# Two graph-attention layers: early row gathers for two chunks, and layer 2 in rounds with one hold of GpSimd

## The chip, the cores and the metric

One core of a Trainium2 chip runs the kernel. Its engines are TensorE (PE, with its weight loads PEld), VectorE (DVE), ScalarE (ACT), GpSimd (POOL) and SyncE (SP); 16 DMA engines move data. The metric is the device time of one execution in microseconds, the median of several.

## The reference

A graph has N = 6250 nodes with 128 features and E = 106250 edges, sorted by destination. Two transformer convolutions with H = 2 heads are computed, with a batch norm and a relu between them, then a residual and a layer norm:

```python
rel_t_enc = jnp.cos((last_update[src] - t)[:, None] * time_w + time_b)
edge_attr = jnp.concatenate([rel_t_enc, msg], axis=-1)        # 32 + 64
def conv(h, ...):
    q, k, v = h @ Wq + bq, h @ Wk + bk, h @ Wv + bv           # (n, 2, 64) each
    e = edge_attr @ We
    alpha = sum(q[dst] * (k[src] + e)) / sqrt(64)             # for each edge and head
    a = exp(alpha - max over dst) / (sum over dst)
    return segment_sum((v[src] + e) * a, dst) + h @ Ws + bs
h = relu(batchnorm(conv(x)))
return layernorm(x + conv(h))
```

## The kernel before

The edges are cut into NC = 104 chunks of 1024 (T = 8 tiles of 128), and each layer goes over the chunks once. A **plan** stage first makes tables of the indices (the source columns `srcs`, the destination columns, the weight columns), checks that the input has the form that the fast path wants, writes the features with their node times as rows `xv_d` to DRAM, and makes block 0 of the tables of layer 1 (`ftab`: query times key weight for each node and head, L630, L636, L638). Then **layer 1**, the statistics of the batch norm, and **layer 2** run, both through the function `conv`.

A chunk passes these stages. *fetch* (SP's queue): attributes of the edges (L781), the four pieces of the table for the chunk's nodes (L797), and others (L803 to L807), behind up to four register loads (L777). *gather* (POOL): 8 indirect DMAs, one for each tile of 128 source rows (L815), from `xv_d` in layer 1 and from `hn_d` in layer 2. *encode* (layer 1): the cosines of the edge's times on DVE and ACT (L853 to L872). *turn_in*: PE transposes the rows (L885, in layer 1 the attributes too, L894), ACT copies them out (L889, L895). *score*: products with the table (L916). *lowest*: DVE finds the greatest exponent (L924, L926). *weigh*: ACT's exp (L931). *turn_weights*: 3 transposes (L940) and a copy (L941). *gather_sums*: 24 matmuls add the weighted rows up (L956) into the bank `fpa`, which comes from a pool of two. *divide*: DVE (L963 to L968). *finish_turn*: two matmuls (L978, L979) into the other half of the same bank and a copy `fat` (L981). *product*: with the value weights (L987, L988; in layer 2 L993, L994), into that half again. *complete*: the residual (L1032, reading `fpa`) and the layer norm (L1032 to L1043); *store* scales the rows (L1049) and sends them out (L761).

The order on every engine is the order of the code. A round k of layer 2 holds, on PE: score(k), product(k-3), turn_weights(k-1), finish_turn(k-2), turn_in(k+1), a piece of other work (later blocks of tables, L630, or of the features, L1219, or the residual, L1299), gather_sums(k-1). DVE does divide(k-2), lowest(k), complete(k-3) and the copy of the time attributes (L1141); ACT does weigh(k) and the copies. The 8 gathers of chunk k+3 are spread over the round: each has a hold, a wait for a step of PE that stands close before it in the code (`behind`, L817 to L819): the end of gather_sums, the score, turn_weights, finish_turn, the two halves of turn_in, and two steps within gather_sums. A gather's rows go into a buffer `ff` of a pool (7 in layer 1, 6 in layer 2). Layer 1 has the same rounds with a lead of four chunks.

Before layer 1's first round, `turn_features` (L656 to L662) transposes all features, 49 transposes in 13 blocks, into `xT`. The first gathers wait for the writing of `xv_d`.

Of the kernel before, what the change touches and what calls it, by code (L numbers as in the profile page):

```python
# [7 lines left out]
F32 = mybir.dt.float32  # L8
# [56 lines left out]
SWITCH = NC - 3  # L65
STARTS = (*range(0, NC - 2, LG), NC - 2, NC - 1)
# [3 lines left out]
def general(ctx: ExitStack, tc: tile.TileContext, x, src, dst, edge_attr_64, edge_weight, node_vec,  # L70
# [95 lines left out]
    step = RW * GT * (-(-64 // GT))  # L166
# [147 lines left out]
    def conv(c, kv_d, qt_d, agg_d):  # L314
        we = wt[c][4]
        w = 2 * D + (c == 1)
        with ExitStack() as cs:
            load = cs.enter_context(tc.tile_pool(name=f"load{c}", bufs=3))
# [217 lines left out]

def room(nc, pl, const, c, w, brief=None):
# [108 lines left out]
def turn_features(nc, pl, mp, N):  # L646
# [5 lines left out]
    for b0 in range(0, NF, 4):  # L652
        n = min(4, NF - b0)
        px = mp.tile([P, 4, P], F32, name="fpx")
        for i in range(n):
            nc.tensor.transpose(px[:, i], pl.rows[:, b0 + i, 1:], pl.ident)  # L656
        eng = nc.scalar.copy if b0 // 4 % 2 else nc.vector.tensor_copy
        eng(lanes[:, b0:b0 + n], px[:, :n])
    if N > NF * P:
        px = mp.tile([P, 4, P], F32, name="fpx")  # L660
        nc.tensor.transpose(px[:, 0], pl.rest[:, 1:], pl.ident)
        nc.vector.tensor_copy(xT[:, NF * P:N], px[:, 0, :N - NF * P])  # L662
# [3 lines left out]
def ordered(ctx: ExitStack, tc: tile.TileContext, pl, x, dst, edge_attr_64, conv2, bn_g, bn_b, out):  # L666
# [9 lines left out]
    const = ctx.enter_context(tc.tile_pool(name="fconst", bufs=1))  # L676
    dram = ctx.enter_context(tc.tile_pool(name="fdram", bufs=1, space=bass.MemoryType.DRAM))
# [51 lines left out]
    AHEAD = 4  # L729

# [9 lines left out]
    def conv(c, extra, first_blocks=None):  # L740
# [9 lines left out]
        p_a = cs.enter_context(tc.tile_pool(name=f"fp_a{c}", bufs=2, space=bass.MemoryType.PSUM))  # L750
        pl.bank = lambda: p_tr.tile([P, GE], F32, name="fpg", tag="tr")

        together = mybir.DependencyInfo(mybir.DependencyClass.Sync, mybir.DependencyReason.DATA)
# [14 lines left out]
        def fetch(k):  # L768
# [9 lines left out]
            s.f = f = load.tile([P, T, FW], F32, name="ff")  # L778
# [22 lines left out]
            if c:  # L801
# [4 lines left out]
                s.r = load.tile([NN, D], F32, name="fr", bufs=7)  # L806
# [3 lines left out]
        def gather(k, rows, behind=None):  # L810
            f = ch[k].f
            for t in rows:
# [31 lines left out]
        def encode(k):  # L844
# [8 lines left out]
            nc.vector.tensor_sub(rel, s.f[:, :, 0], pl.ew[:, :, k])  # L853
# [90 lines left out]
        def gather_sums(k):  # L944
# [3 lines left out]
            s.po = bank[:, 1].rearrange("p (i n) -> p i n", i=2)  # L948
# [35 lines left out]
        def product(k):  # L984
            po, at = ch[k].po, ch[k].at
            if c == 0:
                nc.tensor.matmul(po[:, 0], wv[c], at[:, 0], start=True, stop=False)  # L987
                nc.tensor.matmul(po[:, 0], web[c], at[:, 1], start=False, stop=True)  # L988
                return
            at = at.rearrange("p i (n h) -> p i n h", h=H)  # L990
            for h in range(H):
                r = slice(h * C, (h + 1) * C)
                nc.tensor.matmul(po[:NN, 0, r], at[:, 0, :, h], wv[c][:, r], start=True, stop=False)  # L993
# [566 lines left out]
```

## Time and profile before

| | us |
|---|---|
| median of 3 runs (lowest, highest) | 2671.73 (2668.62, 2673.74) |
| the profiled execution | 2670.95 |
| its span, first to last instruction | 2669.1 |
| granted TensorE clock, mean | 0.879 |
| first gather | 33.6 |
| first score of layer 1 | 87.1 |
| first gather of layer 2 | 1351.4 |
| last lowest (L924) of layer 2 | 2650.7 |

In the profile's lines, an engine's line of code, operation and tiles come first (`ff<-hn_d,fsrcs` writes ff from hn_d by the indices fsrcs). In a group stand the count, the busy time in all, the mean time of one in ns, and the idle time of the engine ahead of these instructions with what ended it. On a timeline stand the start, the time, the engine and the instructions, and in brackets the idle time before; "issue" means that nothing that the profile shows was waited for. A row of a stretch has the busy time of PE, PEld, DVE, ACT and POOL, then the granted clock, the share of the DMA engines and GB/s.

### The profile page before, as it was taken

The numbers are of one execution on the slowest core, as the hardware profiler recorded it, in microseconds if no ns is written. First come the engines' busy times: TensorE is split into PE (matmuls) and PEld (weight loads), VectorE is DVE, ScalarE is ACT, GpSimd is POOL, SyncE is SP. The second block draws the span as 40 slices with busy tenths as digits, with TensorE's granted clock in tenths as the row PEclk, the third lists the DMA queues.
The fourth block names the chain that finished last, engine by engine and source line by source line (L and its number), as shares of the span: only waits on it lengthen the run. The fifth ranks groups of instructions, "written<-read, shape, count | busy, mean of one in ns | idle before, by whom it ended". The sixth has DMA issues, their size and how long they took to land. (4 is left out here: it accounts for less than half of the span.)

```text
span 2669.1 us, 50291 instructions
## 1 busy us (share of the span) xinstructions
PE 1851.4 (69%) x14961; PEld 1107.9 (42%) x14961; DVE 1148.0 (43%) x3998; ACT 1082.5 (41%) x1906; POOL 1588.3 (60%) x1684
## 2 busy tenths in 40 slices
PE   3677767777777677677746667676767767676666
PEld 2444444444444444444424334444444434443443
DVE  3555555555555555565625222333232322232223
ACT  1455545553434444454532333333333333333333
POOL 4466666666666666666345666666666666666662
PEclk8799889988989989889977888888888898888888
DMA  6455555555555555555447555555555555555542
GB/s 177 128 148 146 146 153 145 144 143 151 146 147 138 152 148 145 144 144 138 126 118 194 148 140 148 152 153 147 143 150 148 157 147 142 154 143 140 128 134 52
DMA packets 535244, 383.29 MB, mean 144 GB/s; under 512 B 405638, under 2 KB 479258, under 8 KB 531634
## 3 DMA queue, kind: packets, MB, share of 16 engines
q1 hardware_dynamic: 460998, 231.66, 33.4%
q0 software_dynamic: 53184, 109.45, 17.1%
q10 hardware_dynamic: 20780, 38.87, 3.9%
q8 instruction: 122, 2.00, 0.3%
q14 instruction: 160, 1.31, 0.2%
HBM read 267.85 MB, written 108.49 MB: 141 GB/s over the span
## 5 line engine op out<-in xcount | busy, mean ns | idle before, releaser
L815 POOL DMA_INDIRECT ff<-xv_d,fsrcs x831 | 795.1, 957 | 511.2 <-issue 166.2
L815 POOL DMA_INDIRECT ff<-hn_d,fsrcs x783 | 743.6, 950 | 453.3 <-issue 172.3
L941 ACT COPY fpt<-fppt 128x384 f32<-128x384 f32 x208 | 99.6, 479 | 1261.9 <-PE fpx L885 705.6
L916 PE MATMUL fps<-fft,ftab 128*32 128x384 f32 (+2 forms) x2080 | 406.2, 498 | 146.5 <-issue 64.5
L956 PE MATMUL fpa<-ff,fpt 128*32 128x225 f32 x5008 | 350.6, 419 | 120.0 <-DVE fres L1032 102.2
L924 DVE TENSOR_REDUCE flow<-fps 128x1 f32<-128x384 f32 x208 | 116.1, 558 | 587.6 <-PE fpx L885 352.7
L885 PE MATMUL fpx<-fident,ff 128*128 128x128 f32 x1664 | 276.9, 299 | 38.5 <-issue 25.8
L956 PEld LDWEIGHTS fpa<-ff,fpt 128*32 128x32 f32 x5008 | 167.6, 125 | 321.0 <-issue 233.7
L916 PEld LDWEIGHTS fps<-fft,ftab 128*32 128x32 f32 x2080 | 142.7, 124 | 323.6 <-issue 161.8
L894 PE MATMUL fpe<-fident,ff 128*112 128x128 f32 x832 | 142.4, 295 | 189.0 <-issue 184.3
L889 ACT COPY fft<-fpx 128x512 f32<-128x512 f32 x404 | 232.2, 575 | 45.7 <-remote 20.1
L885 PEld LDWEIGHTS fpx<-fident,ff 128*128 128x128 f32 x1664 | 221.0, 156 | 54.5 <-issue 36.1
L916 PE MATMUL fps<-fxT,ftab 112*32 112x384 f32 (+2 forms) x1040 | 218.4, 509 | 17.2 <-issue 16.8
L963 DVE TENSOR_SCALAR finv<-fpa 128x1 f32<-128x1 f32 x208 | 32.0, 154 | 446.8 <-PE fps L916 237.6
L916 PE MATMUL fps<-fet,ftab 112*32 112x384 f32 (+2 forms) x1040 | 167.4, 448 | 33.0 <-issue 32.7
L894 PEld LDWEIGHTS fpe<-fident,ff 128*112 128x112 f32 x832 | 97.1, 141 | 218.6 <-issue 213.1
L978 PE MATMUL fpa<-fsel,fa 128*128 128x128 f32 x416 | 103.3, 332 | 81.5 <-DVE fsel L968 46.5
L860 DVE SCALAR_TENSOR_TENSOR farg<-fturns,farg 128x256 f32<-128x256 f32 x312 | 132.9, 426 | 10.7
L895 ACT COPY fet<-fpe 112x512 f32<-112x512 f32 x208 | 124.6, 599 | 9.9 <-PE fps L916 2.8
L940 PE MATMUL fppt<-fident,fs 128*128 128x128 f32 x626 | 117.1, 296 | 13.4 <-issue 5.8
L931 ACT ACTIVATE fs<-fps,fm 128x384 f32<-128x384 f32 x208 | 120.5, 579 | 9.7 <-DVE fm L926 6.1
L867 ACT ACT_TABLE_LOAD x82 | 105.2, 1283 | 42.2 <-issue 34.7
(224 smaller groups left out, 2654.4 us busy)
## 6 DMA issues: line engine op xcount, KB each, us to landing
ff<-in_edge_attr SPq DMA_DIRECT2D x206, 256.0 KB
et_d<-fet SPq DMA_DIRECT2D x104, 448.0 KB
fxT<-et_d SPq DMA_DIRECT2D x104, 448.0 KB
tab_d<-fo ACTq DMA_DIRECT2D x26, 1024.0 KB
ftab<-tab_d SPq DMA_DIRECT2D x832, 32.0 KB
enc_d<-fzs SPq DMA_DIRECT2D x104, 128.0 KB
fz<-enc_d SPq DMA_DIRECT2D x104, 128.0 KB
ff<-xv_d,fsrcs POOLq DMA_INDIRECT x831
```

The costliest lines, as they stand in the source:

```text
L815: row = nc.gpsimd.indirect_dma_start(out=f[:, t, (1 if c else 0):1 + D], out_offset=None, in_=(h_d[:N, :] if k < RAW else hn_d) if c else ...
L860: nc.vector.scalar_tensor_tensor(arg, turn, -part, arg, op0=OP.mult, op1=OP.add)
L867: nc.scalar.activation(z[:, :len(of)], arg[:, :len(of)], AF.Sin, bias=qpi)
L885: last = nc.tensor.transpose(px[:, t * P:(t + 1) * P], s.f[:, u * 4 + t, 1:1 + D], ident)
L889: nc.scalar.copy(s.ft[:, u * GE:(u + 1) * GE], px)
L894: last = nc.tensor.transpose(pe[:EC, t * P:(t + 1) * P], s.f[:, u * 4 + t, 1 + D:], ident)
L895: nc.scalar.copy(s.et[:, u * GE:(u + 1) * GE], pe[:EC])
L916: steps.append(nc.tensor.matmul(s.ps[r, to:to + n], s.tab[:kd, r, i], (of.et if i else of.ft)[:kd, at:at + n], start=i == 0, stop=i == 1))
L924: nc.vector.tensor_reduce(low, s.ps, AX.X, OP.min)
L931: nc.scalar.activation(s.s[:, :s.ps.shape[1]], s.ps, AF.Exp, bias=s.bias, scale=-1.0)
L940: last = nc.tensor.transpose(pp[:, t * P:(t + 1) * P], s.s[:, t * P:(t + 1) * P], ident)
L956: steps.append(nc.tensor.matmul(s.pa[r], s.pt[:, t * P + g * GH:t * P + (g + 1) * GH], f[:, i % T, 1:1 + D + EW], start=t == 0, stop=t == ...
```

## The change

**First part: the start.** The 16 gathers of chunks 0 and 1 take their rows directly from the input `x` into two buffers that are kept (`ffe`), as soon as the source columns are there. These rows have no node time in them, so `early_times` works the times out: the source index is split into a slot of 64 nodes and a place in it; a wide matmul spreads the indices over the partitions, ACT and DVE make a one-hot of the slot, four narrow matmuls fetch the slot's 64 times, and DVE picks the place. It stands between the steps of the tables' block 0. The check of the plan comes earlier, and a set of columns comes last. `turn_features` is now taken in pieces by layer 1: 3 blocks in each of the two rounds before the first score and 7 in round 0. In layer 1, gathers up to round 2 have no holds.

On PE this is the start of the program before, from the transpose of the features' first block to the first score (`fx`: features of block 0, `fm`, `fws`: weights of the tables, `fhT`: the features as loaded).

```order
L1513 MATMUL fpx<-fident,fx_234 128x128 x4
L630 MATMUL fpx<-fxT_318,fm_273 128x512
L630 MATMUL fpx<-fxT_318,fm_281 128x512
L630 MATMUL fpx<-fxT_318,fm_289 128x512
L630 MATMUL fpx<-fxT_318,fm_297 128x512
L630 MATMUL fpx<-fxT_318,fws_107 128x512
L1433 MATMUL fpx<-fident,erows 128x104 x8
L1525 COMPARE_AND_BRANCH
L656 MATMUL fpx<-fident,fhT 128x128 x48
L661 MATMUL fpx<-fident,fxrest 128x128
L885 MATMUL fpx<-fident,ff 128x128 x4
```

And on PE after, first the plan from its last table step, then the first stages of layer 1 (`ffe`: the rows gathered from x).

```order
L567 MATMUL fpx<-rowf,frow 98x512
L573 MATMUL fpx<-fslots,fnear 128x64 x4
L673 MATMUL fpx<-fxT_336,fws_109 128x512
L1544 MATMUL fpx<-fident,erows 128x104 x8
L1544 MATMUL fpx<-fident,rowf 128x104 x8
L1646 COMPARE_AND_BRANCH
L699 MATMUL fpg<-fident,fhT 128x128 x12
L935 MATMUL fpx<-fident,ffe_75 128x128 x4
L944 MATMUL fpe<-fident,ffe_75 112x128 x4
L699 MATMUL fpg<-fident,fhT 128x128 x12
L966 MATMUL fps<-fft,ftab 32x384 x4
```

The steps of the early times (L567, L573) stand between those of the tables (L673, before L630), and of the features' 49 transposes (L699, before L656) 24 stand ahead of the first score (L966, before L916).

**Second part: layer 2.** For rounds 0 to 96 the new function `steady` takes every stage's input from a round before: in round k, PE does gather_sums(k-2), score(k), product(k-4), a piece of other work, turn_weights(k-1), finish_turn(k-3), turn_in(k+1); DVE does lowest(k-1), divide(k-3), complete(k-5), and the copy of the attributes last; ACT does weigh(k-1). `catch_up` then does the stages that lag, and the last rounds run in nearly the old order. The bank `fpa` of gather_sums comes from a pool of one in layer 2, and finish_turn and product use a bank `fpo` of their own. The `ff` are a ring of 7, shared by both layers, with the two `ffe` in it.

On PE this is a round of layer 2 before, from the end of the score(k):

```order
L916 MATMUL fps<-fxT,ftab 32x256
L993 MATMUL fpa<-fwv_121,fat 64x64
L994 MATMUL fpa<-fwe_124,fat 64x64
L993 MATMUL fpa<-fwv_121,fat 64x64
L994 MATMUL fpa<-fwe_124,fat 64x64
L940 MATMUL fppt<-fident,fs 128x128 x3
L978 MATMUL fpa<-fsel,fa 128x128
L979 MATMUL fpa<-fsel,fa 128x128
L885 MATMUL fpx<-fident,ff 128x128 x8
L1299 MATMUL fpg<-fws_125,fhT 128x128 x4
L956 MATMUL fpa<-ff,fpt 32x225 x12
```

And a round after, from the end of the score to gather_sums of the next round:

```order
L966 MATMUL fps<-fxT,ftab 32x256
L1044 MATMUL fpo<-fwv_125,fat 64x64
L1045 MATMUL fpo<-fwe_128,fat 64x64
L1044 MATMUL fpo<-fwv_125,fat 64x64
L1045 MATMUL fpo<-fwe_128,fat 64x64
L1407 MATMUL fpg<-fws_129,fhT 128x128 x4
L990 MATMUL fppt<-fident,fs 128x128 x3
L1029 MATMUL fpo<-fsel,fa 128x128
L1030 MATMUL fpo<-fsel,fa 128x128
L935 MATMUL fpx<-fident,ff_470 128x128 x8
L1007 MATMUL fpa<-ffe_76,fpt 32x225
L1007 MATMUL fpa<-ff_468,fpt 32x225 x11
```

The row of matmuls is nearly the same; what moved is the chunk that each belongs to, the piece of other work (L1299, after L1407), and that product and finish_turn (`fpo`) no longer share gather_sums' bank (`fpa`).

On POOL, this is one chunk's gathers before, each with the semaphores that it waits for (`DMASW`: an earlier gather's landing; `PE`: its hold):

```order
L815 DMA ff<-hn_d,fsrcs 128x128 [waits DMASW7_49,DMAHW4_49,DVE_49,PE_49]
L815 DMA ff<-hn_d,fsrcs 128x128 [waits DMASW0_49,PE_49]
L815 DMA ff<-hn_d,fsrcs 128x128 [waits DMASW1_49,PE_49]
L815 DMA ff<-hn_d,fsrcs 128x128 [waits DMASW2_49,PE_49]
L815 DMA ff<-hn_d,fsrcs 128x128 [waits DMASW3_49,PE_49]
L815 DMA ff<-hn_d,fsrcs 128x128 [waits DMASW4_49,PE_49]
```

And one chunk's gathers after:

```order
L865 DMA ff_469<-hn_d,fsrcs 128x128 [waits DMASW7_49,PE_49]
L865 DMA ff_469<-hn_d,fsrcs 128x128 [waits DMASW0_49]
L865 DMA ff_469<-hn_d,fsrcs 128x128 [waits DMASW1_49]
L865 DMA ff_469<-hn_d,fsrcs 128x128 [waits DMASW2_49]
L865 DMA ff_469<-hn_d,fsrcs 128x128 [waits DMASW3_49]
L865 DMA ff_469<-hn_d,fsrcs 128x128 [waits DMASW4_49]
```

Only the first gather of a chunk still waits for PE: the last transpose of turn_in in the round before. The core of the diff:

```diff
+STEADY = NC - 8
+EARLY = 2
-def turn_features(nc, pl, mp, N):
+def turn_features(nc, pl, N):
...
-            s.f = f = load.tile([P, T, FW], F32, name="ff")
+            s.f = f = pl.ffs[k % len(pl.ffs)]
...
+            if not c and k < EARLY:
+                return
...
-            s.po = bank[:, 1].rearrange("p (i n) -> p i n", i=2)
+            s.po = joined[:, :2] if c else bank[:, 1].rearrange("p (i n) -> p i n", i=2)
+            s.product = joined[:NN, 2] if c else s.po[:, 0]
...
+        def steady(k, held):
+            fetch(k + lead(k))
+            gather(k + lead(k), range(T), held)
+            if on(k - 1):
+                lowest(k - 1)
+            if on(k - 3):
+                divide(k - 3)
+            if on(k - 1):
+                weigh(k - 1)
+            if on(k - 5):
+                complete(k - 5)
+            if on(k - 2):
+                gather_sums(k - 2)
+            score(k)
+            if on(k - 4):
+                product(k - 4)
...
+            if on(k - 1):
+                turn_weights(k - 1)
+            if on(k - 3):
+                finish_turn(k - 3)
+            turn_in(k + 1, 0)
+            held = turn_in(k + 1, 1)
...
+            attributes(k)
+            if done:
+                store(*done.pop(0))
+            return held
+
+        def catch_up(k):
+            lowest(k)
+            weigh(k)
+            for j in (k - 4, k - 3, k - 2):
+                while done:
+                    store(*done.pop(0))
+                if j == k - 2:
+                    divide(j)
+                    finish_turn(j)
+                (complete if j == k - 4 else finish)(j)
+            gather_sums(k - 1)
...
+                if c and 0 <= k <= STEADY:
+                    held = steady(k, held)
+                    if k == STEADY:
+                        catch_up(k)
+                    continue
```

More of the change, by code (lines that the diff above doesn't have):

```diff
@@ L1102, in conv @@
                     lowest(k)
[L1103 removed]
+                if not c and on(k - 3) and k <= SWITCH:
                     complete(k - 3)
@@ L1361, in tile_gnn_resnorm @@
         nc.gpsimd.memset(got.hT[:, N // P * (1 + D):], 0.0)
+        got.early = [keep.tile([P, T, FW], F32, name=f"ffe{k}") for k in range(EARLY)]
         got.rest = keep.tile([P, 1 + D], F32, name="fxrest")
@@ L1505, in tile_gnn_resnorm @@
         nc.vector.tensor_scalar(oki, tot, 0.0, None, op0=OP.is_equal)
-        columns(drows, dsts)
-        for _ in matrices(nc, got, 0, keep, bank, pl):
+        rows(nc.scalar, erows, edge_weight, CE)
+        for _ in made_ready:
             pass
+        next(timed)
         codes(nc, got, keep, mw, bank)
```

133 lines of the change are left out of this document (100 added, 33 removed).

## The prediction

> **What bounds the kernel now.** I read the page first, then the table of stretches, then the groups of instructions and the waits of one long stretch of layer 2, then single rounds on the timeline. The page gives the span and says that no engine is busy all the time.
>
> ```profile
> span 2669.1 us, 50291 instructions
> PE 1851.4 (69%) x14961; PEld 1107.9 (42%) x14961; DVE 1148.0 (43%) x3998; ACT 1082.5 (41%) x1906; POOL 1588.3 (60%) x1684
> ```
>
> The run that was profiled took 2670.95 us, 1.85 more than its span, and lies 0.78 below the median of 2671.73. I make the sum against 2670.95 and add the 0.78 at the end. Layer 2 is even in itself, as this stretch of 300 us shows (busy PE, PEld, DVE, ACT, POOL, then clock, DMA share and GB/s):
>
> ```profile
> 1700.00:2000.00 300.00, 209.20 (x1715) 124.49 (x1716) 89.14 (x360) 106.29 (x228) 185.94 (x197) 0.88 0.56 148
> ```
>
> PE is busy 70% and POOL 62%, and DVE, ACT and the DMA engines have room. What a round costs on each engine is in the groups between 1450 and 2600 us:
>
> ```profile
> L815 POOL DMA_INDIRECT ff<-hn_d,fsrcs x756 | 717.3, 949 | 433.3 <-issue 166.1 <-PE fps L916 89.9 <-remote 58.4
> L924 DVE TENSOR_REDUCE flow<-fps 128x1 f32<-128x384 f32 x94 | 52.4, 558 | 243.4 <-PE fpx L885 125.7 <-PE fpg L630 49.4 <-remote 41.5
> L916 PE MATMUL fps<-fft,ftab 128*32 128x384 f32 (+1 forms) x939 | 206.1, 508 | 104.5 <-issue 37.1 <-ACT fspare L1042 26.9 <-ACT fft L889 23.2
> L916 PE MATMUL fps<-fxT,ftab 112*32 112x128 f32 (+2 forms) x943 | 200.7, 504 | 16.8 <-issue 16.3
> L956 PE MATMUL fpa<-ff,fpt 128*32 128x225 f32 x2256 | 145.9, 391 | 118.6 <-DVE fres L1032 101.4 <-issue 16.8 <-DVE fmean L1033 0.4
> L885 PE MATMUL fpx<-fident,ff 128*128 128x128 f32 x752 | 125.4, 318 | 12.0 <-issue 7.4 <-PE fpa L979 2.1 <-DMA ff<-hn_d,fsrcs 1.3
> L993 PE MATMUL fpa<-fwv,fat 128*64 128x64 f32 x376 | 64.0, 246 | 33.9 <-issue 33.2
> L994 PE MATMUL fpa<-fwe,fat 128*64 128x64 f32 x376 | 57.4, 237 | 29.1 <-issue 29.1
> ```
>
> flow stands once in a round, so 94 rounds took 1150 us: **12.23 us a round**. A round holds 8 gathers of 0.949 us busy. Between two gathers that wait for nothing lie 0.30 us (the timeline below), so 8 gathers need 8 x 1.25 = 10.0 us, and 2.2 us of the round are GpSimd waiting, mostly for the step of PE behind which a gather is held. PE in turn idles in front of gather_sums (118.6 us, of which 101.4 for fres, the last reader of the bank) and of the score (104.5 us). So neither engine is full. They wait for each other in turn, and that is what one hold with stages a round apart could take out: at most 2.2 us a round.
>
> **What speaks for a smaller gain.** PE does not work at one speed. This is a quiet round, from 2042.8 us, with GpSimd waiting at its end (PE first, then POOL):
>
> ```profile
> 2042.80 0.33 PE L993 MATMUL fpa<-fwv,fat 128*64 128x64 f32 x2
> 2043.21 0.28 PE L994 MATMUL fpa<-fwe,fat 128*64 128x64 f32 x2
> 2044.26 1.04 PE L885 MATMUL fpx<-fident,ff 128*128 128x128 f32 x8
> 2045.22 1.35 PE L956 MATMUL fpa<-ff,fpt 128*32 128x225 f32 x24
> ```
>
> Product, turn_weights, finish_turn and turn_in follow each other without a gap and are done in 2.5 us. Now the same work in the round after, beside nine gathers without a pause and a tenth:
>
> ```profile
> 2045.72 1.06 POOL L815 DMA_INDIRECT ff<-hn_d,fsrcs  x1 [2.21 <-PE fpx L885]
> ...
> 2055.83 0.94 POOL L815 DMA_INDIRECT ff<-hn_d,fsrcs  x1 [0.30 <-issue]
> 2057.68 0.94 POOL L815 DMA_INDIRECT ff<-hn_d,fsrcs  x1 [0.92 <-issue]
> 2060.72 0.94 POOL L815 DMA_INDIRECT ff<-hn_d,fsrcs  x1 [2.10 <-PE fpx L885]
> ```
> ```profile
> 2056.01 0.37 PE L885 MATMUL fpx<-fident,ff 128*128 128x128 f32 x1 [1.06 <-issue]
> 2056.72 0.37 PE L885 MATMUL fpx<-fident,ff 128*128 128x128 f32 x1 [0.34 <-issue]
> 2058.14 0.37 PE L885 MATMUL fpx<-fident,ff 128*128 128x128 f32 x1 [1.04 <-issue]
> ```
>
> Transposes that wait for nothing ("issue") start 0.7 or 1.4 us apart instead of 0.13, and GpSimd then waits 2.10 us for the last of them. A product of 8 matmuls shows the same where it begins late in a run of gathers; this one, 4.6 us into the run that began at 2072.71, takes 3.24 us to its last start, against 0.47 above:
>
> ```profile
> 2077.32 0.33 PE L993 MATMUL fpa<-fwv,fat 128*64 128x64 f32 x2
> 2078.41 0.29 PE L994 MATMUL fpa<-fwe,fat 128*64 128x64 f32 x2 [0.76 <-issue]
> ...
> 2080.55 0.27 PE L994 MATMUL fpa<-fwe,fat 128*64 128x64 f32 x1 [0.45 <-issue]
> ```
>
> So from about the fourth gather of an unbroken run on, PE's sequencer gets its instructions slowly. How slowly on the whole, the groups of L993 and L994 tell: 33.9 + 29.1 = 63 us of idle time, in 94 products, of which I counted 33 on the timeline that begin in the fourth or fifth gather of a run. 63/33 = 1.9 us each and the 0.47 are 2.4 us, **0.3 us a matmul**; the transposes above are at 0.7. Why, the trace does not say. Today the holds break runs up. The change makes all runs eight long.
>
> **The change, part by part.**
>
> *Layer 2, 97 rounds.* No stage is removed; each round has the same matmuls, gathers and loads, so the worth is in waits alone. Let the hold fall at 0, behind the last transpose. gather_sums has one bank now and must wait until divide of the chunk before has read it. DVE runs, behind finish_turn, the copy fat, the attributes, flow with fm, and three steps of divide:
>
> ```profile
> L981 DVE COPY fat<-fpa 128x256 f32<-128x256 f32 x94 | 37.9, 403 | 2.7 <-PE fpx L885 1.6 <-PE fpg L630 0.8 <-PE fpa L956 0.4
> L1141 DVE COPY ff<-fz 128x256 f32<-128x256 f32 x95 | 27.7, 291 | 0.0
> L966 DVE TENSOR_SCALAR fa<-fpa,finv 128x225 f32<-128x225 f32 x94 | 42.6, 454 | 3.3
> L963 DVE TENSOR_SCALAR finv<-fpa 128x1 f32<-128x1 f32 x94 | 14.9, 158 | 404.2 <-PE fps L916 215.9 <-remote 132.5 <-PE fpa L994 46.3
> ```
>
> 0.40 + 0.29 + 0.56 + 0.45 + three small ones of 0.16 = 2.2 us, of which turn_in covers 1.0: a wait of 0 to 1.2 us (0 if turn_in is slow). Then gather_sums 1.2 us (next start less own) and the score, 20 matmuls of (206.1 + 200.7)/1882 = 0.22 us, so about 2.2 to 4.3 us; with its inputs a round old I take the lower end, since its waits for fft and fspare go. That is 3.4 to 4.6 us into the run of gathers, the point from which PE slows. What is left is product 8, turn_weights 3, finish_turn 2 and turn_in 8 matmuls, 21, and in most rounds one or two of the tables of later rows, 23 in all: 3 us at the quiet rate, 23 x 0.3 = 7 us at the slow one, 16 us at 0.7. Round by the three: 10.0 (GpSimd is longer), 10.4 to 11.6, and above 19, which the end of the gathers at 10.0 cuts off, since PE then speeds up again. The trace has one direct likeness, the run above: 8 x 1.25 and a wait of 2.10 in place of the gap of 0.30 is 11.8. I take **11.6**, near the likeness and the top of the middle. 97 x (11.6 - 12.23) = **-61 us**. Bounds: 10.0 (-216) and 13.1 (+84, below). The gathers that lose their holds cost nothing themselves. Other queues are spared: SP's loads keep three rounds of lead, and the seven row buffers are free two rounds before they are gathered into.
>
> DVE's copy of the attributes (L1141) now runs just as the gathers start. The Trainium skill (SBUF — State Buffer, Who interferes with whom) says that such a DVE copy locks GpSimd out while it runs; by that rule up to 0.29 us a round, 28 us, would be added. The 756 gathers average 949 ns with 95 such copies among them, so the sum has nothing for it.
>
> *The start.* Before, the 28 gathers from 33.6 us on run unbroken while the turned features are made, and PE stops in the middle of them:
>
> ```profile
> 33.61 1.11 POOL L815 DMA_INDIRECT ff<-xv_d,fsrcs  x1 [30.16 <-DMA fwv<-in_L_gnn_Wv]
> ```
> ```profile
> 35.59 4.51 PE L630 MATMUL fpx<-fxT,fm 128*128 128x512 f32 x6 [0.78 <-DVE fxT L1515]
> ...
> 68.38 1.97 PE L656 MATMUL fpx<-fident,fhT 128*128 128x128 f32 x8 [17.04 <-issue]
> 73.99 5.38 PE L656 MATMUL fpx<-fident,fhT 128*128 128x128 f32 x24 [3.64 <-ACT fxT L658]
> ...
> 87.12 1.51 PE L916 MATMUL fps<-fft,ftab 128*32 128x384 f32 x8
> ```
>
> With 16 gathers done earlier, the two idle times of 17.04 and 3.64 should go: -20.7. The 25 transposes moved behind the first score are paid there, at no gain or loss. The early times add 4 matmuls as wide as L630's (4.51/6 = 0.75 us each) and 16 narrow ones (0.13 to 0.2), with their DVE steps: 5 to 6 us in a chain where PE is waiting part of the time. I charge 6: **-15 us**. Bounds -21 (hidden) and +6 (the 16 gathers stall the plan instead; the DMA engines are fuller there):
>
> ```profile
> 12.00:33.00 21.00, 9.74 (x45) 7.59 (x45) 12.15 (x59) 2.87 (x7) 0.00 (x0) 1.00 0.89 280
> ```
>
> *Entry and end of layer 2.* Chunks 0 to 3 of layer 2 are gathered without a hold before and in round 0, much as now: 0, give or take 12. The end makes up two more rounds of product, a finish_turn and a gather_sums at once, 0.5 x 2 + 0.4 + 1.2 and their DVE: **+4** (2 to 8).
>
> **The sum.** -61 - 15 + 4 = -72: 2670.95 - 72 = 2599, and 2600 beside the median.
>
> **The rivals.**
>
> *GpSimd sets the pace.* PE is not slowed by runs of eight, or it is ahead by then. For it: the quiet rows need 3.4 + 3 = 6.4 us, far below 10. Against it: the slow rows. At 10.3 us a round (10.0 and 0.3 for the hold) 97 x -1.93 = -187, with -11 for the rest: 2474. The Trainium skill (SBUF — State Buffer, Who interferes with whom) states that a DMA never contends with a compute engine, which would give this time; the transposes 0.7 us apart beside the gathers speak against it here.
>
> *The runs of eight starve PE.* Nothing of the last 23 matmuls gets through before the gathers end, so every round is 10.0 + 23 x 0.13 = 13.1: +84 - 11 = 2744, **slower**. It decides when a round passes 12.23 + 11/97 = 12.34 us, that is when PE has more than 2.3 us of work left at the last gather. For it: in the run of 28 gathers at the start PE idled 17.04 us, and transposes lay 0.7 us apart already after eight gathers. Against it: the likeness ends at 11.8.
>
> *The rounds gain nothing.* The wait for the one bank and the score's wait for its tables take the place of the holds at 12.2 us; only the start is left: about 2660, and about 2672 if the start, too, pays only by moving its stall into the plan.
>
> **Chances.** Forecast 0.45, GpSimd 0.2, starved 0.22, nothing 0.13 (of which 0.05 within 0.2%, which is about what a measurement of this kernel tells from no change). So faster 0.72, same 0.05, slower 0.23. The likeliest case by itself is 2550 to 2650 (rounds of 11.1 to 12.1). For 8 in 10 the range takes in the GpSimd case's upper part and about half of the starved one: 2470 to 2735.
>
> **What would show it.** Right: runs of exactly 8 gathers in layer 2, then a POOL wait for fpx of 1 to 2 us; flow 11.6 us apart; L956 no longer waiting for fres; the first score near 72 us. Product or turn_in with gaps of "issue" past the fourth gather show the slowing; if these gaps are gone and POOL waits 0.3 us a round, the second case holds. Wrong: POOL waits over 2.5 us a round, or PE waits for a DMA or for SP, of which I charged nothing.

## The result, and the profile after

After took **2860.11 us** (median of 4 runs, 2851.19 to 2865.19) against 2670.57 us for before on the same chip: 1.0705 times as long, 95% interval 1.0687 to 1.0724. The forecast was 2600, the range ended at 2735. The profiled execution of after has a span of 2859.2 us, 190.1 more than before's. The page of after, its span, the busy times and the granted clock in 40 slices:

```profile
span 2859.2 us, 48360 instructions
PE 1887.8 (66%) x15001; PEld 1200.3 (42%) x15001; DVE 1135.8 (40%) x4018; ACT 1094.6 (38%) x1910; POOL 1585.6 (55%) x1684
...
PEclk9799988998898989999677777777777776777777
```

PE and POOL do the same work in a longer time, and the clock is lower from the middle, where layer 2 begins. The stretch that was shown of before, now (busy PE, PEld, DVE, ACT, POOL, then clock, DMA share, GB/s):

```profile
1700.00:2000.00 300.00, 193.79 (x1532) 126.52 (x1528) 75.24 (x320) 98.37 (x206) 166.97 (x177) 0.74 0.49 130
```

177 gathers in 300 us, where before had 197. The length of a round comes from the tile flow (count, min/median/max, first and last start), and GpSimd's time from its groups between 1550 and 2750 us:

```profile
L974 DVE TENSOR_REDUCE flow<-fps x87: 537/545/547, 1555.3 to 2745.4; 128x1 f32<-128x384 f32 x87
```
```profile
L865 POOL DMA_INDIRECT ff<-hn_d,fsrcs x490 | 462.7, 944 | 375.7 <-PE fpx L935 221.4 <-issue 128.0 <-remote 23.6
L865 POOL DMA_INDIRECT ffe<-hn_d,fsrcs x203 | 191.7, 944 | 171.1 <-PE fpx L935 112.1 <-issue 58.6 <-DMA ffe<-hn_d,fsrcs 0.3
```

86 rounds in 1190.1 us are **13.84 us a round**, against 12.23. The gathers are as long as before, 0.944 us. They idle 546.8 us; 606 gaps of 0.30 inside the chunks are 182, so 365 us are left for 87 holds, 4.2 us each: 8 x 0.944 + 7 x 0.30 + 4.2 = 13.85. In these 4.2 us is the gap of 0.30 that any gather has ahead of it. Counted as the prediction counts, beyond 8 x 1.25 = 10.0 us, GpSimd now waits 3.8 us in a round, where before it waited 2.2. One round shows where the time goes (POOL, then PE):

```profile
1996.74 0.94 POOL L865 DMA_INDIRECT ff<-hn_d,fsrcs  x1 [3.38 <-PE fpx L935]
...
2005.47 0.94 POOL L865 DMA_INDIRECT ff<-hn_d,fsrcs  x1 [0.30 <-issue]
2011.33 0.94 POOL L865 DMA_INDIRECT ff<-hn_d,fsrcs  x1 [4.91 <-PE fpx L935]
```
```profile
2002.06 0.34 PE L1044 MATMUL fpo<-fwv,fat 128*64 128x64 f32 x2
...
2003.21 0.22 PE L1045 MATMUL fpo<-fwe,fat 128*64 128x64 f32 x1 [0.45 <-issue]
2003.92 0.26 PE L1045 MATMUL fpo<-fwe,fat 128*64 128x64 f32 x1 [0.49 <-issue]
...
2006.75 0.27 PE L990 MATMUL fppt<-fident,fs 128*128 128x128 f32 x1 [0.72 <-issue]
2007.47 0.32 PE L990 MATMUL fppt<-fident,fs 128*128 128x128 f32 x1 [0.45 <-issue]
2008.17 0.31 PE L990 MATMUL fppt<-fident,fs 128*128 128x128 f32 x1 [0.38 <-issue]
2008.27 0.65 PE L1029 MATMUL fpo<-fsel,fa 128*128 128x128 f32 x2
...
2009.14 1.91 PE L935 MATMUL fpx<-fident,ffe 128*128 128x128 f32 x8
```

The product starts 5.3 us after the first gather. Its first six matmuls keep their pace, and the last two start 0.7 us apart. The three transposes of turn_weights, with nothing to wait for, lie 0.7 us apart too, and all three start after the last gather has ended (2006.41). From 2008.27 on, 1.9 us after that end, the gaps are gone, but PE is not back at full pace: turn_in takes 1.91 us, where the same eight transposes took 1.04 in the quiet round of before. The granted clock goes with it: 0.50 here and 1.00 there (a stretch of after, then one of before, in the columns used above):

```profile
2009.10:2011.00 1.90, 1.90 (x10) 1.55 (x8) 1.51 (x8) 1.44 (x3) 0.00 (x0) 0.50 0.59 142
```
```profile
2044.20:2045.20 1.00, 1.00 (x10) 0.85 (x9) 0.90 (x6) 0.41 (x1) 0.00 (x0) 1.00 0.29 78
```

The hold falls at 2011.33. The gaps are no matter of this round alone: from the product to turn_in, PE idled 277 us in these 87 rounds without waiting for anything that the profile shows, 3.2 us a round. In 86 rounds of before (1550 to 2600 us) the same stages have 84 us of it, 1.0 us a round.

The start did not get shorter either. PE, from the first step of the tables on:

```profile
40.98 2.08 PE L673 MATMUL fpx<-fxT,fm 128*128 128x512 f32 x2 [0.78 <-DVE fxT L1629]
42.99 2.02 PE L567 MATMUL fpx<-rowf,pones 1*98 1x512 f32 x2
46.39 1.97 PE L573 MATMUL fpx<-fslots,fnear 98*128 98x64 f32 x8 [1.38 <-DVE fnear L570]
48.15 2.02 PE L673 MATMUL fpx<-fxT,fm 128*128 128x512 f32 x2
...
70.20 2.02 PE L673 MATMUL fpx<-fxT,fws 128*128 128x512 f32 x2
...
90.07 0.85 PE L966 MATMUL fps<-fft,ftab 128*32 128x384 f32 x8
...
91.50 0.66 PE L935 MATMUL fpx<-fident,ffe 128*128 128x128 f32 x4
107.94 1.07 PE L944 MATMUL fpe<-fident,ffe 128*112 128x128 f32 x4 [15.79 <-issue]
```

The first score starts at 90.07 us (before 87.12). The first step of the tables comes 5.4 us later than before (40.98 against 35.59). The block of the tables, 35.6 to 42.5 before, now lasts from 41.0 to 72.2. In it stand 8 wide and 32 narrow matmul records of the early times, in four passes of 7 to 8 us; they took 15.8 us of PE, and PE idled 6.2 us ahead of them. The ten records of the tables themselves took 10.1 us instead of 6.6. Then the stop of PE is back, 15.79 us beside a run of 24 gathers from 76.6 to 106.5, so the first lowest falls at 110.7 (before 90.2) and the last of layer 1 at 1350.6 (before 1334.4).

### The profile page after: what moved, and what is told of

Read it like the earlier page. It is cut to its first block, busy times and chain, and to the rows that moved or that the text cites. A ratio compares the mean times of both kernels' runs of the same rounds, so it can differ in the third digit from the quotient of the medians.

```text
span 2859.2 us, 48360 instructions
## 1 busy us (share of the span) xinstructions
PE 1887.8 (66%) x15001; PEld 1200.3 (42%) x15001; DVE 1135.8 (40%) x4018; ACT 1094.6 (38%) x1910; POOL 1585.6 (55%) x1684
## 4 chain that ended last, share of the span: by engine, by line
PE 48%; issue 22%; DVE 13%; another core or an unknown queue 8%; ACT 5%; DMA 2%; SPq 1%; POOL 0%; DVEq 0%; ACTq 0%; POOLq 0%
PE fps L966 11%; PE fpa L1007 10%; PE fpx L935 5%; PE fpg L673 4%; PE fpe L944 3%; PE fppt L990 3%; DVE fa L1017 2%; PE fpo L1044 2%; DVE flow L974 2%; PE fpo L1030 1%; PE fpo L1045 1%; DVE fat L1032 1%; PE fpo L1029 1%; PE fpa L1029 1%
## 5 line engine op out<-in xcount | busy, mean ns | idle before, releaser
L865 POOL DMA_INDIRECT ff<-hn_d,fsrcs x559 | 529.6, 947 | 452.4 <-PE fpx L935 243.7
L865 POOL DMA_INDIRECT ff<-xv_d,fsrcs x591 | 564.7, 956 | 352.8 <-issue 123.3
L966 PE MATMUL fps<-fft,ftab 128*32 128x384 f32 (+2 forms) x2080 | 326.8, 518 | 49.8 <-issue 27.5
L865 POOL DMA_INDIRECT ffe<-hn_d,fsrcs x224 | 212.3, 948 | 185.6 <-PE fpx L935 120.5
L865 POOL DMA_INDIRECT ffe<-xv_d,fsrcs x224 | 214.0, 955 | 162.3 <-PE fps L966 58.7
L935 PE MATMUL fpx<-fident,ff 128*128 128x128 f32 x1184 | 221.8, 325 | 43.2 <-issue 34.9
L1007 PE MATMUL fpa<-ffe,fpt 128*32 128x225 f32 x1444 | 141.0, 475 | 88.0 <-DVE fa L1017 81.1
L966 PEld LDWEIGHTS fps<-fft,ftab 128*32 128x32 f32 x2080 | 132.4, 134 | 149.6 <-issue 75.5
L966 PE MATMUL fps<-fet,ftab 112*32 112x384 f32 (+2 forms) x1040 | 173.0, 451 | 28.9 <-issue 28.4
L966 PE MATMUL fps<-fxT,ftab 112*32 112x384 f32 (+2 forms) x1040 | 158.4, 496 | 1.4 <-issue 1.4
L681 DVE SCALAR_TENSOR_TENSOR fo<-fpg,fb,fcode 128x512 f32<-128x512 f32 x50 | 57.2, 1147 | 235.5 <-remote 91.0
L679 ACT ACTIVATE fo<-fpg,fb 128x512 f32<-128x512 f32 x50 | 59.3, 1191 | 195.4 <-PE fpg L673 89.6
```

Of the source, the lines that this page charges most:

```text
L865: row = nc.gpsimd.indirect_dma_start(out=f[:, t, (1 if c else 0):1 + D], out_offset=None, in_=(h_d[:N, :] if k < RAW else hn_d) if c else ...
L935: last = nc.tensor.transpose(px[:, t * P:(t + 1) * P], s.f[:, u * 4 + t, 1:1 + D], ident)
L966: steps.append(nc.tensor.matmul(s.ps[r, to:to + n], s.tab[:kd, r, i], (of.et if i else of.ft)[:kd, at:at + n], start=i == 0, stop=i == 1))
L1007: steps.append(nc.tensor.matmul(s.pa[r], s.pt[:, t * P + g * GH:t * P + (g + 1) * GH], f[:, i % T, 1:1 + D + EW], start=t == 0, stop=t == ...
```

## The experiments

**Theory A**: an unbroken run of gathers starves the other engines of instructions, and this alone makes the rounds longer. **Rival B**: the new order does it, with one bank, DVE's chain ahead of gather_sums and one hold. Each kernel was run beside before on its own chip; before took 2671 us on two of these, 2704 and 2707 on two others, and 2208 on a fifth, so that only ratios within one chip are compared.

**The parts apart.** The start alone is after with the old layer 2:

```diff
-                if c and 0 <= k <= STEADY:
-                    held = steady(k, held)
...
-            s.po = joined[:, :2] if c else bank[:, 1].rearrange("p (i n) -> p i n", i=2)
+            s.po = bank[:, 1].rearrange("p (i n) -> p i n", i=2)
```

> The first part of the change alone: the early gathers and the new start of after, and layer 2 as in before (holds for every gather, two banks). Theory A (unbroken runs of gathers slow every engine): the start still costs what it costs in after, the first lowest about 20 us later than before, and layer 2 goes back to 12.2 to 12.5 us a round; 2670 + 16 to 20 = about 2688. Rival B (the order of the stages, with one bank and DVE's chain in front of gather_sums, makes the rounds of 13.8 us): the same number here, about 2688, since the order is that of before. Rival C (the ring of seven shared buffers makes the layers wait for each other): rounds above 13 us stay, about 2800.

Measured: 2676.87 against 2671.17 us, ratio 1.0026 (1.0014 to 1.0038). Layer 2 is back at 12.1 us a round, against C. The first lowest is late, at 112.4 us, but the end is only 8.6 us late in the profile: the start costs some 6 us by the medians, less than any theory gave it.

Layer 2 alone has the start of before and `steady` and `catch_up` of after.

> The second part of the change alone: the start as in before, layer 2 as in after (and the ring of buffers). Theory A, on a chip with the slowing: after less its start, 2860 - 8 to 16 = about 2848. On a chip without it: after less 16 to 20 us of the start, which puts it at or a little below before, 2170 to 2230. Rival: the same distance from before as after.

Measured: 2854.56 against 2671.08 us, 1.0677 (1.0642 to 1.0713). After itself on the same chip:

> After, unchanged. The last runs were on a chip on which before took 2208 us and no engine slowed beside long runs of gathers; the earlier ones on a chip with 2671 us and the slowing. Theory A says that the change's loss is this slowing alone. So on a chip with it: 2860 beside 2671 as before. On a chip without it: rounds of layer 2 of 10.1 to 10.4 us, 8 gathers at 1.25 us and a short wait, and the start some 15 us later; beside 2208 that is -1 to +2 per cent, 2190 to 2250. Rival (the order with one hold is slower anyhow): over 2330 there.

Measured: 2848.93, 1.0663 (1.0645 to 1.068). So layer 2 holds the whole loss.

**One hold or the order.** Before, with one hold for each chunk and the order as it was:

```diff
                 elif not filling:
-                    bring(range(1), ended)
+                    bring(range(T if c else 1), ended)
+                if c and k >= 0:
+                    coming = []
```

> Before with one edit: in layer 2 all eight gathers of a chunk stand at the start of a round behind one hold (the end of gather_sums of the round before), the order of the stages as it was. Theory A: rounds of 13.5 us or more, PE with gaps of 0.7 us from about the fourth gather on: 2670 + 97 x 1.3 = about 2800 or more. Rival B: rounds stay at 12.2, about 2670, since order and banks are those of before.

Measured: 2845.61, 1.0638 (1.0575 to 1.0702). Its gathers between 1550 and 2750 us:

```profile
L815 POOL DMA_INDIRECT ff<-hn_d,fsrcs x695 | 656.8, 945 | 541.3 <-PE fpa L956 340.1 <-issue 186.8 <-remote 11.0
```

695 gathers in 1200 us are 13.8 us a round, as in after, in the old order and with two banks. The one hold is enough. The place of the loss is another, though, than the expectation said:

```profile
L956 PE MATMUL fpa<-ff,fpt 128*32 128x225 f32 x2064 | 222.7, 534 | 413.1 <-ACT fpt L941 183.5 <-issue 167.9 <-DVE fat L981 61.6
```

Product to turn_in, which stand early in the run here, have no idle time at all; PE idles 413 us in front of gather_sums, late in the run: 183.5 of them for ACT's copy fpt and 167.9 for nothing that the profile shows. That ACT is late because it, too, gets its instructions slowly is argued, not shown. The other way round, after with its order and the holds spread again:

```diff
-            gather(k + lead(k), range(T), held)
+            gather(k + lead(k), (0,), held)
...
+            gather(k + lead(k), (3,), half)
+            gather(k + lead(k), (4,), scored)
```

> After with one edit: in steady the eight gathers are spread over the round again, each behind a step of TensorE (the last transpose, the fourth matmul and the end of gather_sums, the two halves of the score, turn_weights, finish_turn, the first half of turn_in). Theory A: rounds of 12.2 us or less, so that 2860 goes down by 97 x 1.6 or more, to 2700 or less. Rival B: the rounds keep 13.5 to 13.8 us, about 2850.

Measured: 2685.45, 1.0058 (1.0036 to 1.008), and between 1550 and 2600 us:

```profile
L865 POOL DMA_INDIRECT ff<-hn_d,fsrcs x485 | 458.3, 945 | 284.9 <-issue 107.9 <-PE fps L966 76.3 <-remote 51.7
L865 POOL DMA_INDIRECT ffe<-hn_d,fsrcs x202 | 190.6, 944 | 117.0 <-issue 48.7 <-remote 30.0 <-PE fps L966 25.7
```

687 gathers in 1050 us: 12.2 us a round. The idle time of PE that waits for nothing goes with the loss, as turn_weights shows (after, then this kernel):

```profile
L990 PE MATMUL fppt<-fident,fs 128*128 128x128 f32 x261 | 66.5, 334 | 60.6 <-issue 60.3
```
```profile
L990 PE MATMUL fppt<-fident,fs 128*128 128x128 f32 x258 | 46.2, 290 | 0.4 <-issue 0.4
```

The holds take all but 14 us of the loss back, and the order by itself gives nothing. B falls.

**The slowing by itself.** A kernel that only copies x out runs PE through 280 transposes that wait for nothing, ten times, beside other work:

```python
for g in range(G):                       # GpSimd
    gather(g)
for i in range(TP):                      # TensorE
    nc.tensor.transpose(banks[i // 4 % 4][:, i % 4], gate, ident)
```

> Not the kernel but a measurement: it computes nothing of the reference (it copies x out). Ten stretches, in each of which TensorE does 280 transposes that wait for nothing, beside GpSimd doing: nothing; 24 gathers of 128 rows of 512 bytes; 24 gathers of 128 rows of 16 bytes; 24 gathers of 32 rows of 512 bytes; 24 plain DMAs of 128 rows from GpSimd's queue; 24 such DMAs from SyncE's queue; 40 memsets; 12 gathers with two memsets between each; 24 gathers and 24 DMAs of SyncE; nothing. Theory A1 (the work of issuing a gather hinders the supply of instructions): a transpose takes 0.11 us alone and several times that in the later part of both stretches with 128-row gathers, with 16-byte rows as with 512-byte rows, and stays at 0.11 beside SyncE's DMAs and memsets. Theory A2 (the moved bytes hinder it): slow with 512-byte rows from either queue, 0.11 us with 16-byte rows. Theory A3 (only together with loads from SyncE's queue): slow in the ninth stretch alone. Rival B (no hindrance; PE in the kernel waits for something that the trace does not show): 0.11 us everywhere.

The first 7.5 us of a stretch and what follows while GpSimd is busy (busy PE, PEld, DVE, POOL with counts, clock, DMA share, GB/s): gathers of 512-byte rows, of 16-byte rows, of 32 rows, then SyncE's DMAs, memsets, and gathers with two memsets between.

```profile
38.20:45.70 7.50, 7.50 (x69) 7.50 (x70) 0.00 (x0) 5.80 (x6) 1.00 0.18 46
45.70:68.20 22.50, 8.53 (x44) 5.47 (x42) 0.00 (x0) 17.01 (x19) 0.68 0.20 52
...
101.10:123.60 22.50, 7.45 (x39) 4.93 (x37) 0.00 (x0) 17.02 (x18) 0.66 0.06 2
...
156.60:176.60 20.00, 5.17 (x23) 2.74 (x21) 0.00 (x0) 14.82 (x18) 0.66 0.06 14
...
236.90:254.90 18.00, 17.98 (x165) 17.98 (x166) 0.00 (x0) 0.00 (x0) 1.00 0.33 88
268.10:290.90 22.80, 22.80 (x209) 22.80 (x210) 0.00 (x0) 20.56 (x40) 1.00 0.01 1
299.30:326.80 27.50, 27.50 (x252) 27.50 (x253) 0.00 (x0) 24.12 (x36) 1.00 0.11 30
```

Alone, PE does 9.2 transposes in a microsecond. Beside gathers without a pause it does so for 7.5 us and then 44 in 22.5 us. With rows of 16 bytes, when the DMA engines are busy 6%, it is 39, and with 32 rows 23 in 20 us. SyncE's plain DMAs, memsets and spaced gathers leave it alone, and so do GpSimd's plain DMAs (274 in 30 us in the next measurement). Gathers and SyncE's DMAs together (55.8 us for the 280) are little worse than gathers alone (54.8). So it is neither the bytes nor the DMA engines, and smaller rows or fewer of them do not help; it is the gather instructions in close order. A2, A3 and B fall. Two repeats on other chips gave the same within a few per cent:

> The first measurement again, unchanged. On a chip with the slowing: as before, 280 transposes in 55 us beside 24 gathers against 30.5 alone. On the other chip theory A expects 30.5 us in all stretches; the rival that only the kernel differs there (another clock, or other loads) expects 55 us.

> The first measurement beside it. On a chip without the slowing 30.5 us for 280 transposes in every stretch after the first, if theory A is right that the two chips differ in this; on the others 55 us beside the unbroken gathers.

280 transposes beside unbroken 512-byte gathers took 54.4 us on the one and 55.0 on the other, 30.5 alone on both. Both were chips with the slowing.

How far apart must gathers be? The same with a memset behind each gather:

> A measurement, not the kernel (it copies x out and computes nothing else). As before, stretches of 280 transposes that wait for nothing, now beside: nothing; 24 gathers with a memset of 32, 128, 256, 384 or 512 columns behind each, which spaces them 1.3 to 1.9 us apart; 72 plain DMAs of GpSimd; runs of 8 gathers with a pause of about 2.2 us; runs of 4 with about 1.1 us; 24 gathers without pause beside 70 wide matmuls in place of the transposes; nothing. Theory A (each gather needs some 1.45 us of a service that the engines' instruction supply shares, and a backlog of it starves them; 1.45 from PE's recovery 40.4 us after the first of the 28 gathers that started at 33.6 us in before): no slowing from a spacing of about 1.5 us on, slowing below; in runs of 8 with a pause of 2.2 us little or none; none beside plain DMAs. Rival (a fixed number of gathers in a run starts it, whatever their spacing): slow in the last five gathers of each spacing below 2 us, none in runs of 4. The wide matmuls, with a quarter of the instructions, start to slow later than the transposes' 9 us if engines live from instructions fetched ahead, and at the same time if not.

The later part of each stretch, with gathers 1.26, 1.34 and 1.45 us apart, the whole of one with 1.55, then the wide matmuls beside gathers without pause:

```profile
46.20:68.70 22.50, 7.69 (x45) 5.41 (x43) 0.00 (x0) 19.53 (x37) 0.68 0.20 52
...
101.70:126.70 25.00, 13.96 (x73) 10.17 (x72) 0.00 (x0) 21.69 (x38) 0.64 0.18 48
...
163.70:180.70 17.00, 16.02 (x115) 12.34 (x114) 0.00 (x0) 15.16 (x24) 1.00 0.17 46
182.30:212.30 30.00, 29.99 (x275) 30.00 (x276) 0.00 (x0) 26.63 (x39) 1.00 0.17 43
...
374.00:394.00 20.00, 20.00 (x48) 8.83 (x47) 0.00 (x0) 15.12 (x17) 1.00 0.20 52
```

In a microsecond 2.0, 2.9, 6.8 and 9.2 transposes: the edge lies between 1.45 and 1.55 us a gather. The runs of 8 and of 4 did not stand each beside a stretch of its own, because the plain DMAs ahead of them outlasted theirs: the 280 transposes that took 35.0 us ran beside two runs of 8, with pauses of 2.4 us, and two runs of 4. They slowed for about two microseconds at the end of each run of 8 (15 transposes in the 2.5 us from 319.9) and not beside the runs of 4 (97 in 10.4 us). In the kernel the slowing starts earlier, 6.5 us after a run's first gather; why is open.

The wide matmuls were not slowed at all: beside the 24 gathers PE started 70 of them and 69 loads, 139 instructions, while the transposes of the first measurement lost their pace after 75 to 89 of them and as many loads, 150 to 178. That would fit engines that live from instructions fetched ahead until these run out, but the record speaks against the simplest form of it. The profile's instruction queue q8 moved 22 packets of 16 KB for the 5600 instructions of PE in the first measurement, one for about 255, and it moved one at 44 us, just ahead of the slow part. From there to 72 us PE started 115 instructions and the queue moved none. So PE slowed while, by this count, it had not yet used up what that packet brought; where the supply is held up stays open.

**What the rounds of before are made of.** The kernel of the start alone, every other gather of layer 2 left out:

```diff
-                if k == NC - 1 and t > whole:
+                if k == NC - 1 and t > whole or c and t % 2:
                     continue
```

> The kernel of the start alone (old layer 2 with its holds), with every other gather of layer 2 left out, so that half of its rows are stale and the output is not the reference's; all other instructions stay. Theory A (GpSimd's gathers can be served at one each 1.45 to 1.5 us, and the rounds of 12.1 us in all these kernels are 8 of them): rounds of layer 2 fall to what PE needs, 8.4 to 9 us as in the last rounds of layer 1, where no gathers are left: 2677 - 100 x 3.2 = about 2350. Rival (the chain of PE, DVE and ACT sets 12.1 us, and the gathers only fill in): rounds of 11.5 us or more, above 2600.

Measured: 2288.65, 0.8583 (0.8556 to 0.861).

```profile
1500.00:1800.00 300.00, 249.46 (x2485) 158.92 (x2484) 133.54 (x527) 157.18 (x334) 136.97 (x144) 0.93 0.70 183
```

144 gathers, 4 a round: 8.3 us a round, with all matmuls, loads and copies in it. So the chain of PE, DVE and ACT needs 8.3 us at most, and the other four gathers, with their holds, make 12.1 of it. Since to take the holds away made the rounds longer, this points to the gathers and not the holds: 12.1 us are about 1.5 us for each of eight, the edge that the transposes show.

**Gathers spaced in the kernel.** After, and before with one hold, with memsets of 256 or 352 columns:

```diff
+                if c and k >= 3:
+                    nc.gpsimd.memset(pl.ew.rearrange("p t k -> p (t k)")[:, :256], 0.0)
```

> After with one addition: in layer 2 GpSimd does a memset of 256 columns behind each gather, so that the gathers of a run stand 1.45 us apart, as measured, and not 1.25. The one hold and the order stay, and GpSimd has more to do. Theory A: a run of eight no longer outruns the service, PE is not starved, and a round takes 8 x 1.45 = 11.6 to 12.2 us: 2860 - 97 x 1.7 to 2.2 = 2645 to 2695. Rival (one hold a round costs the time, however the gathers are spaced): a round of 13.9 us plus the 1.6 us of memsets, or 13.9 at least: 2860 to 3010.

> The same with memsets of 352 columns, gathers some 1.52 us apart. Theory A: no backlog at all, rounds of 12.2 to 12.4 us: about 2695 to 2720, a little more than with 1.45. Rival: 2860 or more.

> The kernel with one hold in the old order (13.8 us a round, 2846) with the same memsets of 256 columns. Theory A: 11.6 to 12.4 us a round, 2640 to 2710. If the order of the stages a round apart is worth something once PE is not starved, this one is slower a round than after with the same memsets; if not, the same. Rival: 2846 or more.

These three ran on the chip on which before takes 2208.1 us: 2371.32 (1.0738, 1.0718 to 1.0759), 2436.2 (1.1032, 1.1013 to 1.105) and 2362.33 (1.0698, 1.068 to 1.0715). In the unpaced layer 1 of the first of them:

```profile
300.00:600.00 300.00, 230.59 (x2097) 168.09 (x2097) 194.53 (x656) 173.68 (x261) 228.01 (x237) 0.85 0.65 169
```

237 gathers in 300 us are 1.27 us each, 10.1 us a round, in a run of 775 without a pause, and PE did 2097 matmuls beside them (in before on the first chip 196 and 1801 in that stretch). The start of this kernel is that of after, and behind the first score PE does not stop here, beside the same unbroken gathers:

```profile
85.64 0.66 PE L937 MATMUL fpx<-fident,ffe 128*128 128x128 f32 x4
86.14 0.60 PE L946 MATMUL fpe<-fident,ffe 128*112 128x128 f32 x4
```

These are the two rows that lie 16.4 us apart in after. The tables, too, start at 35.78 us here and not at 40.98. This chip has no slowing to take away, so the memsets only cost time: 11.5, 12.1 and 11.6 us a round, what the gathers and memsets themselves take. The kernel again, on a chip with the slowing:

> After with memsets of 256 columns behind each gather of layer 2 (1.45 us apart), which the last call ran on the chip without the slowing (11.41 us a round, 2371 beside 2208). On a chip with the slowing theory A expects rounds of 11.6 to 12.2 us, 2645 to 2695 beside 2671, against 13.9 without the memsets; the rival 13.9 or more. On a chip without it: 2371 again.

Measured: 2715.35 against 2671.08, 1.0156 (1.0138 to 1.0173), where after took 2848.93. Rounds of 12.4 us and not 13.8, with more work for GpSimd: spacing alone takes three quarters of the loss back, and A stands, though the rounds are longer than the 11.6 to 12.2 us that it gave. Smaller spacing should have been better still, in layer 2, and in both layers with one hold:

> Layer 2 as in after, the start as in before, and a memset of 128 columns behind each gather of layer 2: 1.34 us apart. Theory A with a service of 1.45 us: a run of eight takes 10.7 us and leaves a backlog of 8 x 0.11 = 0.9 us only, so PE slows little at the end of a run; rounds of 11.6 to 12.0 us: 2671 - 97 x 0.25 to 0.6 = 2610 to 2650, faster than both kernels. If the slowing needs only a short excess, rounds of 12.4 or more: 2690 or more. On a chip without the slowing (before at 2208): GpSimd sets 10.7 to 11 us, slower than before, about 2290.

> Before with one hold a round (the end of gather_sums) in both layers in place of the eight, the old order, and a memset of 128 columns behind each gather of chunk 5 and later. Theory A: 11.6 to 12.2 us in both layers, 2671 less 0 to 100 = 2570 to 2670. If the old order needs the holds' small pauses, 12.5 or more, above 2700. On a chip without the slowing 10.8 to 11.2 us a round, 2300 to 2380.

Both missed: 2840.69 against 2704.1 (1.0513, 1.0486 to 1.054) with rounds of 13.7 us, and 3072.72 (1.1355, 1.1336 to 1.1373) with 13.6 in layer 2 and 14.8 in layer 1. On this chip after took 14.1 us a round. At 1.34 us a run of eight slows PE nearly as much as at 1.25. My picture of a service of 1.45 us with a backlog, harmless while small, is wrong in its second half.

After ran twice more, both times on a chip with the slowing:

> After, unchanged, once more, for the chip without the slowing. There theory A expects rounds of layer 2 of 10.1 to 10.5 us and 2190 to 2250 beside 2208; the rival (one hold and the order cost the time on any chip) over 2330. On a chip with the slowing: 2850 to 2860 beside 2671.

> After, unchanged, tried once more for a chip on which nothing slows beside the gathers. There, by theory A, 2190 to 2250 beside 2208; by the rival over 2330. On a chip with the slowing, 2840 to 2910 again, which tells nothing new.

2906.66 against 2704.1 (1.0756, 1.0737 to 1.0775) and 2913.05 against 2707.09 (1.0754, 1.0729 to 1.0779). What the change does on a chip without the slowing stays open. No version beat before on a chip with it.

## Why the prediction was wrong

**What bounds the kernel now** is the step that failed first. I read POOL at 62% as room and the 2.2 us of waiting in a round as up for taking. The spread holds in the new order (12.2 us a round) and the half gathers (8.3 us) show otherwise: at 8 gathers a round and about 1.5 us each the old kernel is at the edge, and the waits at the holds act as the spacing that keeps PE fed. Taken away in either order, they cost 1.6 us a round here and gained nothing. The prediction's own sign of being wrong came with it: POOL waited 333.5 us for the last transpose (fpx) in 87 rounds, 3.8 us a round, where over 2.5 was to mean wrong.

**The round of 11.6 us** is the step that failed by number: 13.84 measured, 97 x 2.24 = 217 us more than the sum. The mechanism was in the text, PE slowed from about the fourth gather on, and the row is as I read it. The size came from one likeness, a run that GpSimd left with a wait of 2.10 us; over 87 holds of after it is 4.2 us. The sum let PE return to full pace when the gathers end. In the round shown the gaps lasted 1.9 us longer, and turn_in then took another 0.9 us more than at the quiet rate, at half the granted clock, a cost that the sum does not have. The starved rival had the place and the sign right and the same fault in its price: 13.1.

**The wait for the one bank**, 0 to 1.2 us, came out above its upper end: PE waited 118.2 us for fa in these 87 rounds, 1.4 us a round. How much of that is DVE being fed slowly itself is not shown. Rows free, SP's lead: nothing charged, and neither shows among the longer waits.

**The start**, forecast at -15: +6 us by itself. The two idle times did not go; a run of 24 gathers put a stop of 15.79 us behind the first score. The early times, charged with 6, made the block of the tables 24 us longer. The step that failed is the count: 4 wide and 16 narrow matmuls of the code were charged at the price of one record in the trace, but each of them is two records. These 40 records took 15.8 us, with 6.2 us of waits. And the 16 early gathers stalled the plan, which was only the bound of +6: the tables start 5.4 us later than in before, and 5.2 later than with the same code on the chip without the slowing. The later stages made more than half of all this up.

**Entry and end of layer 2**, charged with 4 us: from the last lowest of layer 1 to that of layer 2 (2841.1) after takes 174 us more than before, and 97 x 1.61 = 156 of them are the rounds. The 18 us that are left were not taken apart.

**The GpSimd rival** (2474) fell with its rule. The Trainium skill (SBUF — State Buffer, Who interferes with whom) says that a DMA never contends with a compute engine; here 44 transposes instead of 207 in 22.5 us beside gathers speak against using it as a bound for indirect DMAs, though no row shows that an SBUF port is what they contend for, and rows of 16 bytes do it too. That the copy of the attributes locks GpSimd out cost after nothing, but it was hardly put to the test: of 44 copies between 1550 and 2150 us only 14 ran beside a gather, and these gathers took 0.944 us, the others 0.942. In before the mean of 949 ns hid that it does happen: between 1450 and 2050 us, 44 gathers beside such a copy took 0.984 us on average, the longest of them 1.36, and the others 0.945. At one copy a round that is 0.04 us, too little to matter here.

**The chances** gave 0.22 to the starved case. Its evidence, PE idle for 17.04 us beside 28 gathers and transposes 0.7 us apart after eight, was the broader one; the evidence for the likeliest case was one run.

## What to carry to other kernels

Many small waits of one engine in a tuned kernel can be what keeps the others going: before taking holds away, look what the others do where the engine already runs without a pause. A price from one lucky row is worth less than the mean over all rows of its kind, and an experiment that leaves out half of the suspected work (here 12.1 to 8.3 us a round) tells in one run what a stage is bound by.

## What the runs showed of the hardware

- Beside indirect gathers 1.25 us apart, TensorE fell from 9.2 to 2 transposes in a microsecond after 8 to 10 us; at 1.45 us it did 6.8 in the later part, and at 1.55 it was not slowed. Bytes and rows did not matter, and plain DMAs and memsets of GpSimd did not do it. What the gathers and the instruction supply share, the runs do not tell.
- SyncE is held up as well: four loads behind the first score of after took 9.82 us to issue (from 90.77 on), and 2.05 us at the same place on the chip without the slowing.
- Five chips of the experiments took 2208, 2671, 2671, 2704 and 2707 us for the same kernel; on the first the slowing is missing, and rounds of layer 1 took 10.1 us, the gathers' own time. Whether a ratio measured on one chip holds on another was not measured: after itself never ran on the first.
- Slowed, PE also drops in granted clock, 0.64 to 0.68 in the two measurements and 0.74 in layer 2 of after (0.88 before), and it can stay low after the gaps: 0.50 for the turn_in shown, whose transposes took 1.91 us instead of 1.04.
